# U3 h computed once in the reset gate's PSUM bank, copied into the update gate's bank, with both gates' message products added on top

## The chip, the cores and the metric

The kernel runs on one core of a Trainium2 chip. The metric is the device time of one execution in microseconds, as the median of several executions. Everything is in one launch; the inputs are `x` (16 x 1024 x 128), a symmetric 0/1 adjacency matrix `adj` (1024 x 1024) and the weights, all fp32.

## The reference, cut to what matters

Layer 0 is a graph attention layer with a residual and a layer normalization; the change doesn't touch it. Layer 1 is a gated graph network: five steps, each of which replaces the state `h` of every batch, and then a residual and a layer normalization.

```python
def step(h, _):
    m_in = jnp.einsum('nm,bmd->bnd', in_matrix, h)      # adj
    m_out = jnp.einsum('nm,bmd->bnd', out_matrix, h)    # adj too: m_in == m_out
    av = jnp.concatenate([m_in, m_out], axis=-1)
    u3 = h @ u3_w.T + u3_b
    z = jax.nn.sigmoid(av @ w3_w.T + w3_b + u3)
    r = jax.nn.sigmoid(av @ w4_w.T + w4_b + u3)
    hv = jnp.tanh(av @ w5_w.T + w5_b + (r * h @ u5_w.T + u5_b))
    h = (1.0 - z) * h + z * hv
```

The term `u3` is the same in both gates.

## The kernel before

**Tiling.** The state of a batch is held transposed, as `hT`: 128 features on the partitions, 1024 nodes along the free axis, worked on in two halves of 512 (`e` = 0, 1). A half is one PSUM bank of 128 x 512 fp32. Since both adjacency matrices are `adj`, the kernel makes `m = adj h` once and adds the two halves of each gate's weight into `wm` (three 128 x 128 blocks: z, r, candidate) at the start. The sigmoids are made as tanh of half the argument, so the tanh takes `scale=0.5` and half the bias (`bh`), and the kernel works with r' = tanh and (r' + 1) h; the missing factor is in `u5h`, half of U5.

**One step of one batch** (`step(b, s)`), for each half, with the lines of the profile:

- L878: 16 products with `adj` add up the message into the bank `ps_acc` (the state, in node order, is split into two parts of a shorter format, `hN`, so that there are 2 x 8 of them); L896: ScalarE copies the bank to SBUF, as `m`.
- L908: the U3 product, from `hT`, into a bank of its own (`ps_g_u`); L911: ScalarE moves it to SBUF as `u`, with the bias of U3 added.
- L918: the message products of r and z from `m`, each into a bank (`ps_g_r`, `ps_g_z`); L921: VectorE adds `u` to each and writes the sum to SBUF; L924: ScalarE takes the tanh, in place.
- L932: VectorE makes (r + 1) h. L938 and L939: TensorE makes the candidate, the message part first and then the part of r h, in one bank (`ps_g_v`); L942: ScalarE takes its tanh, `hv`.
- L949, L956, L963: VectorE makes the new half of `hT` from `hv`, `z` and the old one.
- The new state has to be turned back to node order for the next step. L478: VectorE transposes blocks of 32 x 32; L483: SP's queue issues four DMAs that write it to a buffer D in DRAM, L487: one that reads it back as F; L497 (ScalarE, a cast) and L501 (VectorE, a subtraction) split F into the two parts of `hN` for the next adj products. For the last step of the last three batches, and some tiles of the first two, TensorE transposes instead (L468).

An fp32 product of this size takes two passes on TensorE, an adj product one.

Layer 0 of a batch: products of `x` with the weights (L524), one attention column (`pb`), 8 chunks of weighted sums on VectorE (L678), adj products of their own (L749, L805), a layer normalization (L441 to L455: VectorE, GpSimd, ScalarE), and the same turns through DRAM.

**The order of work** is not written out by hand. Each operation is given to a planner (`Plan.add`) with its engine, a length in nanoseconds, a rank, and what it reads and writes. Ranks come from batch and step (`rank_of(b, s)`: 5b + 3s, with other values for the last two batches, so that about two batches are in their steps at a time and another's layer 0 lies between) plus an offset from the table `D` (for the gates 0.2, for their sums 0.3 and 0.5, for the candidate 0.4, for a split 0.8). `Plan.order()` then plays the engines through, once, when the kernel is built: an engine that is free takes the ready operation of lowest rank for whose tiles there is still a buffer. Buffers are counted by kind in `kinds`; "ps" stands for the eight PSUM banks, shared by all products. The result is one fixed order for each engine, which is emitted as it is. On the chip an engine works through its list strictly in that order, and waits where an input isn't there yet. A change of the planner's operations or buffer counts can therefore move any instruction.

Planned lengths and allowances (`R` an adj product, `F` an fp32 product of 512 columns, `V` a VectorE and `A` a ScalarE operation, in ns):

```python
R, F, TR, V, A = 233, 858, 109, 605, 640
LAG = {"PE": 250, "DVE": 150, "ACT": 170, "POOL": 200, "SP": 2500, "DMA": 2400}
```

At the start TensorE has nothing to do for a few microseconds, and runs `IDLE` = 24 groups of four transposes of the identity (`idle_`, L396), of lowest rank.

Of the kernel before, what the change touches and what calls it, by code (L numbers as in the profile page):

```python
# [9 lines left out]
F32 = mybir.dt.float32  # L10
F32R = mybir.dt.float32r
I32 = mybir.dt.int32
AF = mybir.ActivationFunctionType
ALU = mybir.AluOpType
AX = mybir.AxisListType

P = 128
N = 1024
HALF = 512
# [106 lines left out]
def kernel(  # L126
# [52 lines left out]
    nc = tc.nc  # L179
    B = x_t.shape[0]  # L180

    const = ctx.enter_context(tc.tile_pool(name="const", bufs=1))
    PS = bass.MemoryType.PSUM
# [4 lines left out]
    wm = const.tile([P, 3, P], F32, tag="wm", name="wm")  # L188
    u3 = const.tile([P, P], F32, tag="u3", name="u3")
    u5 = const.tile([P, P], F32, tag="u5", name="u5")  # L190
    u5h = const.tile([P, P], F32, tag="u5h", name="u5h")
    bias = const.tile([P, 5], F32, tag="bias", name="bias")
    bh = const.tile([P, 2], F32, tag="bh", name="bh")
    b5 = const.tile([P, 1], F32, tag="b5", name="b5")
    ident = const.tile([P, P], F32, tag="ident", name="ident")
    shift = const.tile([P, 1], F32, tag="shift", name="shift")
    ones = const.tile([P, 2], F32, tag="ones", name="ones")
    mhalf = const.tile([P, NC], F32, tag="mhalf", name="mhalf")
    att2 = const.tile([P, 2], F32, tag="att2", name="att2")

    seen = const.tile([P, B, NC + 4], F32, tag="seen", name="seen")
# [4 lines left out]
    def exact(pools):  # L206

        def pool(name, bufs, space=None):
# [7 lines left out]
        kinds = {  # L216
            "xt": (2, [P, N], F32, None),
            "hx": (2, [P, NC, P + 3], F32, None),
            "pb": (1, [P, N], F32, None),
            "hl": (2, [P, 2, NC, P], F32R, None),  # L220
            "yT": (1, [P, N], F32, None),
            "part": (1, [P, HALF], F32, None),
            "junk": (1, [P, HALF], F32, None),
            "y0": (4, [P, NC, P], F32, None),
# [2 lines left out]
            "T": (3, [P, HALF], F32, None),  # L227
            "F": (3, [P, HALF], F32, None),
            "m": (4, [P, HALF], F32, None),
            "u": (3, [P, HALF], F32, None),  # L230
            "r": (3, [P, HALF], F32, None),
            "z": (3, [P, HALF], F32, None),
            "hv": (2, [P, HALF], F32, None),
# [10 lines left out]
            "rstd": (3, [P, 2, 4], F32, None),  # L244
            "D": (6, [P, HALF], F32, bass.MemoryType.DRAM),
            "ud": (2, [3, N], F32, bass.MemoryType.DRAM),
            "ps": (8, [P, HALF], F32, PS),
        }
        places = {tag: pool(f"{tag}_p", k[0], k[3]) for tag, k in kinds.items()}
        tiles = {}  # L250
# [1 line left out]
        def T(t, dtype=None, shape=None):  # L252
            if t not in tiles:
                _, sh, dt, _ = kinds[t[0]]
                tiles[t] = places[t[0]].tile(
                    shape or sh, dtype or dt, tag=t[0], name="_".join(map(str, t)).replace("-", "n")
                )
            return tiles[t]
# [14 lines left out]
        R, F, TR, V, A = 233, 858, 109, 605, 640  # L273

        def pe(*a, **k):
            plan.add("PE", *a, **k)

        def dve(*a, **k):
            plan.add("DVE", *a, **k)

        def act(*a, **k):
            plan.add("ACT", *a, **k)
# [5 lines left out]
        D = dict(m=0, pu=0, u=0, pr=0.2, pz=0.2, sr=0.3, r=0.3, pv=0.4, sz=0.5, z=0.5, hv=0.6, h=0.6, tr=0.6, split=0.8)  # L288
# [13 lines left out]
        boot = ("hl", "boot")  # L302
# [5 lines left out]
        ws = ("T", "ws")  # L308
# [40 lines left out]
        def lands(pieces, what):  # L349
            plan.add("DMA", 190 * pieces, -103, lambda: None, writes=what)  # L350
# [7 lines left out]
        for k in range(NC // 2):  # L358
            lands(8, [(staged[k], 1)])
        lands(9, [(boot, "ws"), (("xt", 1), 0), (("xt", 1), 1)])  # L360
        lands(10, [(boot, "late"), (("u",), 0), (ws, "b")])

        def constants():
            make_identity(nc, ident)
            nc.gpsimd.memset(shift, -SHIFT)
            nc.gpsimd.memset(ones, 1.0)
            nc.gpsimd.memset(mhalf, -0.5)

        plan.add("POOL", 2000, -100, constants, writes=[(("ident",), 0), (("ones",), 0)])

# [23 lines left out]
        def idle_():  # L394
            for j in range(4):
                nc.tensor.transpose(T(("ps", "idle"))[:, j * P : (j + 1) * P], ident, ident)  # L396

        for i in range(IDLE):
            pe(4 * TR, 9000, idle_, reads=[(("ident",), 0)], writes=[(("ps", "idle"), 0)])

# [3 lines left out]
        def sums():  # L404
            w = W("w345").rearrange("p (j t e) -> p j t e", j=3, t=2)
            nc.vector.tensor_tensor(wm, w[:, :, 0, :], w[:, :, 1, :], ALU.add)
            nc.vector.tensor_tensor(b5, bias[:, 2:3], bias[:, 4:5], ALU.add)
            nc.vector.tensor_scalar(u5h, u5, 0.5, None, ALU.mult)
            nc.vector.tensor_scalar(bh, bias[:, 0:2], 0.5, None, ALU.mult)

        def own_weights():
            pb_ = ("ps", "g", "b")
            pe(150, -4.6, lambda: column_(pb_, slice(2 * P, 3 * P), 5), reads=[(ws, "b"), (("rz", 0), 1)], writes=[(pb_, 0)])
            dve(160, -4.3, lambda: nc.vector.tensor_copy(bias, T(pb_)[:, 0:5]), reads=[(pb_, 0)], writes=[(("bias",), 0)])
            dve(270, -4.5, self_, reads=[(boot, "ws"), (("ident",), 0), (("zs", 0), NC - 1)], writes=[(("wsi",), 0)])
            dve(1000, -4.2, sums, reads=[(boot, "late"), (("bias",), 0), (("u",), 0), (("rz", 0), 1)], writes=[(("wm",), 0)])

        def adj_tables(c):
            st = staged[c // 2]
# [448 lines left out]
        def step(b, s):  # L868
            rank = rank_of(b, s)
            hT, hN, y0 = ("hT", b), ("hN", b, s), ("y0", b)  # L870
            hs = [slice(0, HALF), slice(HALF, N)]
            for e in range(2):
                pm, m = ("ps", "acc", b, s, e), ("m", b, s, e)

                def pm_(e=e, pm=pm):
# [18 lines left out]
                    writes=[(pm, 0)],  # L894
# [2 lines left out]


            for e in range(2):
                m, u, r, z, hv = (k + (b, s, e) for k in (("m",), ("u",), ("r",), ("z",), ("hv",)))  # L900
                pu, pr, pz, pv = (("ps", "g", b, s, e, k) for k in ("u", "r", "z", "v"))
                mark = (("after",), b, s, e)

                def h(e=e):
                    return T(hT)[:, hs[e]]

                def pu_(pu=pu, h=h):
                    nc.tensor.matmul(T(pu), u3, h(), start=True, stop=True)  # L908

                def u_(pu=pu, u=u):  # L910
                    nc.scalar.activation(T(u), T(pu), AF.Identity, bias=bias[:, 3:4], scale=1.0)  # L911

                pe(F, rank + D["pu"], pu_, reads=[(hT, e), (("u",), 0)], writes=[(pu, 0), mark])
                act(A, rank + D["u"], u_, reads=[(pu, 0), (("bias",), 0)], writes=[(u, 0)])
                for p_, t, j, due in ((pr, r, 1, 'r'), (pz, z, 0, 'z')):

                    def gate_(p_=p_, j=j, m=m):
                        nc.tensor.matmul(T(p_), wm[:, j, :], T(m), start=True, stop=True)  # L918

                    def sum_(p_=p_, t=t, u=u):  # L920
                        nc.vector.tensor_tensor(T(t), T(p_), T(u), ALU.add)  # L921

                    def sig_(t=t, j=j):
                        nc.scalar.activation(T(t), T(t), AF.Tanh, bias=bh[:, j : j + 1], scale=0.5)  # L924

                    pe(F, rank + D["p" + due], gate_, reads=[(m, 0), mark, (("wm",), 0)], writes=[(p_, 0)])
                    dve(V, rank + D["s" + due], sum_, reads=[(p_, 0), (u, 0)], writes=[(t, 0)])
                    act(A, rank + D[due], sig_, reads=[(t, 0)], writes=[(t, 1)])
                dve(
                    V,  # L930
                    rank + D["r"],
                    lambda r=r, h=h: nc.vector.scalar_tensor_tensor(T(r), T(r), 1.0, h(), ALU.add, ALU.mult),  # L932
                    reads=[(r, 1), (hT, e)],
                    writes=[(r, 2)],
                )

                def pv_(pv=pv, m=m, r=r):
                    nc.tensor.matmul(T(pv), wm[:, 2, :], T(m), start=True, stop=False)  # L938
                    nc.tensor.matmul(T(pv), u5h, T(r), start=False, stop=True)  # L939

                def hv_(pv=pv, hv=hv):
                    nc.scalar.activation(T(hv), T(pv), AF.Tanh, bias=b5, scale=1.0)  # L942

                pe(2 * F, rank + D["pv"], pv_, reads=[(m, 0), (r, 2), (("wm",), 0), (("u",), 0)], writes=[(pv, 0)])
                act(A, rank + D["hv"], hv_, reads=[(pv, 0), (("wm",), 0)], writes=[(hv, 0)])
                dve(
                    V,
                    rank + D["h"],
                    lambda hv=hv, h=h: nc.vector.tensor_tensor(T(hv), T(hv), h(), ALU.subtract),  # L949
                    reads=[(hv, 0), (hT, e)],  # L950
                    writes=[(hv, 1)],
                )
                dve(
                    V,
                    rank + D["h"],
                    lambda hv=hv, z=z: nc.vector.scalar_tensor_tensor(T(hv), T(z), 1.0, T(hv), ALU.add, ALU.mult),  # L956
                    reads=[(hv, 1), (z, 1)],
                    writes=[(hv, 2)],
                )
                dve(  # L960
                    V,
                    rank + D["h"],
                    lambda hv=hv, h=h: nc.vector.scalar_tensor_tensor(h(), T(hv), 0.5, h(), ALU.mult, ALU.add),  # L963
                    reads=[(hv, 2)],
                    writes=[(hT, e)],
                )
# [376 lines left out]
```

## Time and profile before

| | before |
|---|---|
| median of 3 executions | 1528.85 us (1527.25 to 1529.43) |
| profiled execution, its own time | 1530.39 us |
| its span in the trace | 1528.6 us |
| granted TensorE clock, mean | 0.993 |
| TensorE (PE) busy | 1497.9 us, 98%, 5200 instructions |
| VectorE (DVE) busy | 1171.3 us, 77%, 2757 |
| ScalarE (ACT) busy | 841.6 us, 55%, 1656 |
| GpSimd (POOL) busy | 141.0 us, 9%, 265 |
| share of the chain that ended last | PE 87%, DMA 4%, DVE 3%, POOL 2%, ACT 2% |

How to read it: the busy time of an engine is the time in which it worked on an instruction, waits not counted. PE is the products and PEld the loading of their weights, which goes on beside them. The span goes from the first to the last recorded event; the execution's own time is 1.79 us longer than the span. The chain is followed backwards from the last instruction, at each step to whatever let it start. In a row of groups, "out<-in" are the tile names without their numbers, then sizes and types, then how many; after the bar stand the group's busy time in us and the mean of one in ns; then the engine's idle time just ahead of it and what ended most of that. In a timeline row stand the start in us, the length in us, engine, line, operation and tiles; SPq is SP's DMA queue.

### The profile page before, as it was taken

To read this page: it belongs to the slowest core of one execution; us is meant where nothing else is said; L and a number is where in the kernel's file an instruction comes from. 1 tells how busy PE (TensorE), PEld (TensorE's weight loads), DVE (VectorE), ACT (ScalarE), POOL (GpSimd) and SP (SyncE) were. 2 spreads that over 40 slices of the span, in tenths; PEclk is the share of its full clock that TensorE was granted. 3 is DMA by queue.
4 is the path that set the end of the run, shared out by engine and by line. 5 is a ranking of instruction groups with operands and counts; after the bars stand their busy time and mean duration, and the time that the engine had idled before them with its cause. 6 is when DMAs were issued, how large, how long until landed. Compare 5 with 4: busy or idle time off the path is not lost.

```text
span 1528.6 us, 17756 instructions
## 1 busy us (share of the span) xinstructions
PE 1497.9 (98%) x5200; PEld 944.5 (62%) x5200; DVE 1171.3 (77%) x2757; ACT 841.6 (55%) x1656; POOL 141.0 (9%) x265
## 2 busy tenths in 40 slices
PE   8999999999999999999999999999999999999996
PEld 7656566666666666666666566666666666666663
DVE  5778787878787777877878778777877888776665
ACT  4564645566465655555566455655555565555544
POOL 0101001011110201111011110101111011000001
PEclk9999999999999999999999999999999999999998
DMA  4124344242433324334242433324334233322121
GB/s 171 30 81 124 89 124 122 87 119 84 117 90 97 104 63 130 85 96 129 67 124 74 118 91 97 104 62 127 88 98 124 64 88 111 104 75 78 42 74 38
DMA packets 193982, 144.83 MB, mean 95 GB/s; under 512 B 33279, under 2 KB 158934, under 8 KB 193878
## 3 DMA queue, kind: packets, MB, share of 16 engines
q1 hardware_dynamic: 193314, 142.78, 32.8%
q8 instruction: 42, 0.69, 0.2%
q10 hardware_dynamic: 564, 0.85, 0.2%
q14 instruction: 62, 0.51, 0.1%
HBM read 79.95 MB, written 63.61 MB: 94 GB/s over the span
## 4 chain that ended last, share of the span: by engine, by line
PE 87%; DMA 4%; DVE 3%; POOL 2%; ACT 2%; SPq 1%; issue 1%; POOLq 0%; DVEq 0%; ACTq 0%
PE ps_acc L878 36%; PE ps_g_r L918 8%; PE ps_g_u L908 8%; PE ps_g_v L938 8%; PE ps_g_v L939 8%; PE ps_g_z L918 8%; PE ps_acc_po L749 7%; PE ps_g_ph L524 1%; DMA F<-D 1%; DMA D<-T 1%; SPq L483 1%; DMA F_y<-D_y 1%; POOL rstd_y L448 1%; PE ps_acc_po L805 1%; ACT y L455 1%
## 5 line engine op out<-in xcount | busy, mean ns | idle before, releaser
L878 PE MATMUL ps_acc<-adj,hN 128*128 128x512 f32 x2560 | 668.9, 415 | 0.7 <-DVE hN L501 0.7
L878 PEld LDWEIGHTS ps_acc<-adj,hN 128*128 128x128 f32 x2560 | 479.9, 188 | 166.9 <-issue 55.2
L896 ACT COPY m<-ps_acc 128x512 f32<-128x512 f32 x160 | 92.9, 580 | 156.7 <-PE ps_acc L878 156.4
L501 DVE TENSOR_TENSOR hN<-F,hN 128x512 fp32r<-128x512 f32 x128 | 88.1, 689 | 116.3 <-ACT hN L497 115.9
L942 ACT ACTIVATE hv<-ps_g_v,b 128x512 f32<-128x512 f32 x160 | 109.8, 687 | 105.5 <-PE ps_g_v L939 105.4
L918 PE MATMUL ps_g_r<-m,wm 128*128 128x512 f32 x320 | 164.4, 595 | 3.6 <-ACT m L896 3.6
L938 PE MATMUL ps_g_v<-m,wm 128*128 128x512 f32 x320 | 164.3, 595 | 3.4 <-ACT u L911 3.4
L939 PE MATMUL ps_g_v<-r,u5h 128*128 128x512 f32 x320 | 164.4, 595 | 0.3 <-DVE r L932 0.3
L918 PE MATMUL ps_g_z<-m,wm 128*128 128x512 f32 x320 | 163.4, 592 | 0.0
L497 ACT CAST hN<-F 128x512 fp32r<-128x512 f32 x128 | 79.1, 619 | 135.5 <-DMA F<-D 135.2
L921 DVE TENSOR_TENSOR r<-ps_g_r,u 128x512 f32<-128x512 f32 x160 | 109.0, 683 | 58.3 <-PE ps_g_r L918 55.0
L908 PE MATMUL ps_g_u<-hT,u 128*128 128x512 f32 x320 | 152.7, 598 | 0.7 <-ACT hT L861 0.7
L924 ACT ACTIVATE r<-r,bh 128x512 f32<-128x512 f32 x160 | 114.8, 721 | 67.5 <-DVE r L921 66.3
L949 DVE TENSOR_TENSOR hv<-hv,hT 128x512 f32<-128x512 f32 x160 | 109.5, 685 | 55.1 <-ACT hv L942 54.3
L749 PE MATMUL ps_acc_po<-adj,hl 128*128 128x512 f32 x512 | 145.5, 432 | 1.8 <-ACT hl L726 1.0
L749 PEld LDWEIGHTS ps_acc_po<-adj,hl 128*128 128x128 f32 x512 | 97.3, 190 | 42.1 <-issue 19.1
L924 ACT ACTIVATE z<-z,bh 128x512 f32<-128x512 f32 x160 | 113.0, 716 | 12.4 <-DVE z L921 11.6
L932 DVE SCALAR_TENSOR_TENSOR r<-r,hT 128x512 f32<-128x512 f32 x160 | 108.5, 681 | 12.7 <-ACT r L924 12.5
L911 ACT ACTIVATE u<-ps_g_u,bias 128x512 f32<-128x512 f32 x160 | 106.1, 682 | 17.5 <-PE ps_g_u L908 17.2
L956 DVE SCALAR_TENSOR_TENSOR hv<-z,hv 128x512 f32<-128x512 f32 x160 | 108.6, 680 | 3.4 <-ACT z L924 0.9
L921 DVE TENSOR_TENSOR z<-ps_g_z,u 128x512 f32<-128x512 f32 x160 | 108.5, 682 | 2.9 <-PE ps_g_z L918 2.0
L939 PEld LDWEIGHTS ps_g_v<-r,u5h 128*128 128x128 f32 x320 | 61.0, 191 | 77.7 <-issue 61.5
(132 smaller groups left out, 1482.5 us busy)
## 6 DMA issues: line engine op xcount, KB each, us to landing
D<-T SPq DMA_DIRECT2D x616, 64.0 KB
F<-D SPq DMA_DIRECT2D x154, 256.0 KB
out_dram<-o SPq DMA_DIRECT2D x32, 256.0 KB
xt<-in_x_dram SPq DMA_DIRECT2D x15, 512.0 KB
pb<-ud SPq DMA_DIRECT2D x14, 512.0 KB
D_y<-T_y SPq DMA_DIRECT2D x112, 64.0 KB
F_y<-D_y SPq DMA_DIRECT2D x28, 256.0 KB
D_b<-T_b SPq DMA_DIRECT2D x112, 64.0 KB
```

The lines of the kernel that those rows point to most:

```text
L749: nc.tensor.matmul(T(po), hl[:, k, c, :], adj[:, c, hs], start=(first and i == 0), stop=(last and i == len(terms) - 1),)
L878: nc.tensor.matmul(T(pm), T(hN)[:, k, c, :], adj[:, c, hs[e]], start=(c == 0 and k == 0), stop=(c == NC - 1 and k == 1),)
L908: nc.tensor.matmul(T(pu), u3, h(), start=True, stop=True)
L918: nc.tensor.matmul(T(p_), wm[:, j, :], T(m), start=True, stop=True)
L921: nc.vector.tensor_tensor(T(t), T(p_), T(u), ALU.add)
L924: nc.scalar.activation(T(t), T(t), AF.Tanh, bias=bh[:, j : j + 1], scale=0.5)
L932: lambda r=r, h=h: nc.vector.scalar_tensor_tensor(T(r), T(r), 1.0, h(), ALU.add, ALU.mult),
L938: nc.tensor.matmul(T(pv), wm[:, 2, :], T(m), start=True, stop=False)
L939: nc.tensor.matmul(T(pv), u5h, T(r), start=False, stop=True)
L942: nc.scalar.activation(T(hv), T(pv), AF.Tanh, bias=b5, scale=1.0)
L949: lambda hv=hv, h=h: nc.vector.tensor_tensor(T(hv), T(hv), h(), ALU.subtract),
L956: lambda hv=hv, z=z: nc.vector.scalar_tensor_tensor(T(hv), T(z), 1.0, T(hv), ALU.add, ALU.mult),
```

## The change

The U3 product of a half goes straight into the bank of the r gate. ScalarE copies it from there into the bank of the z gate; with that the copy to SBUF as `u` and its pool are gone. The message products of r and z no longer start a new sum in their banks (`start=False`), but add to what is there. The two additions on VectorE are removed, and the two tanhs read PSUM. The bias of U3, which the move to SBUF added, is now added to `bh` once at the start.

The z gates get two banks of their own ("gz"), and the common pool "ps" has six in place of eight. [...]two products of the identity with a tile of zeros (`fill_`) are run into the two "gz" banks once at the start, with `start=True`. GpSimd sets that tile of zeros. The r bank is started by the U3 product itself. The message products now also depend on the copy, r's as well as z's.

The table `D`, the planned lengths and everything of layer 0 are as before; only the key of the weights' landing is called "uw" instead of "u".

```diff
             "T": (3, [P, HALF], F32, None),
             "F": (3, [P, HALF], F32, None),
             "m": (4, [P, HALF], F32, None),
-            "u": (3, [P, HALF], F32, None),
...
-            "ps": (8, [P, HALF], F32, PS),
+            "ps": (6, [P, HALF], F32, PS),
+            "gz": (2, [P, HALF], F32, PS),
...
             nc.gpsimd.memset(mhalf, -0.5)
+            nc.gpsimd.memset(zeros, 0.0)
...
+        def fill_(k):
+            nc.tensor.matmul(T(("gz", "fill", k)), ident, zeros, start=True, stop=True)
+
+        for k in range(kinds["gz"][0]):
+            pe(F, -99, lambda k=k: fill_(k), reads=[(("ident",), 0)], writes=[(("gz", "fill", k), 0)])
...
-            nc.vector.tensor_scalar(bh, bias[:, 0:2], 0.5, None, ALU.mult)
+            nc.vector.tensor_tensor(bh, bias[:, 0:2], bias[:, 3:4].to_broadcast([P, 2]), ALU.add)
+            nc.vector.tensor_scalar(bh, bh, 0.5, None, ALU.mult)
...
-                m, u, r, z, hv = (k + (b, s, e) for k in (("m",), ("u",), ("r",), ("z",), ("hv",)))
-                pu, pr, pz, pv = (("ps", "g", b, s, e, k) for k in ("u", "r", "z", "v"))
+                m, r, z, hv = (k + (b, s, e) for k in (("m",), ("r",), ("z",), ("hv",)))
+                pr, pz, pv = ("ps", "g", b, s, e, "r"), ("gz", b, s, e), ("ps", "g", b, s, e, "v")
...
-                def pu_(pu=pu, h=h):
-                    nc.tensor.matmul(T(pu), u3, h(), start=True, stop=True)
-
-                def u_(pu=pu, u=u):
-                    nc.scalar.activation(T(u), T(pu), AF.Identity, bias=bias[:, 3:4], scale=1.0)
-
-                pe(F, rank + D["pu"], pu_, reads=[(hT, e), (("u",), 0)], writes=[(pu, 0), mark])
-                act(A, rank + D["u"], u_, reads=[(pu, 0), (("bias",), 0)], writes=[(u, 0)])
-                for p_, t, j, due in ((pr, r, 1, 'r'), (pz, z, 0, 'z')):
+
+                def pu_(pr=pr, h=h):
+                    nc.tensor.matmul(T(pr), u3, h(), start=True, stop=True)
+
+                def u_(pr=pr, pz=pz):
+                    nc.scalar.copy(T(pz), T(pr))
+
+                pe(F, rank + D["pu"], pu_, reads=[(hT, e), (("uw",), 0)], writes=[(pr, 0), mark])
+                act(A, rank + D["u"], u_, reads=[(pr, 0)], writes=[(pz, 0)])
+                for p_, t, j, due in ((pr, r, 1, "r"), (pz, z, 0, "z")):
 
                     def gate_(p_=p_, j=j, m=m):
-                        nc.tensor.matmul(T(p_), wm[:, j, :], T(m), start=True, stop=True)
-
-                    def sum_(p_=p_, t=t, u=u):
-                        nc.vector.tensor_tensor(T(t), T(p_), T(u), ALU.add)
-
-                    def sig_(t=t, j=j):
-                        nc.scalar.activation(T(t), T(t), AF.Tanh, bias=bh[:, j : j + 1], scale=0.5)
-
-                    pe(F, rank + D["p" + due], gate_, reads=[(m, 0), mark, (("wm",), 0)], writes=[(p_, 0)])
-                    dve(V, rank + D["s" + due], sum_, reads=[(p_, 0), (u, 0)], writes=[(t, 0)])
-                    act(A, rank + D[due], sig_, reads=[(t, 0)], writes=[(t, 1)])
+                        nc.tensor.matmul(T(p_), wm[:, j, :], T(m), start=False, stop=True, skip_group_check=True)
+
+                    def sig_(p_=p_, t=t, j=j):
+                        nc.scalar.activation(T(t), T(p_), AF.Tanh, bias=bh[:, j : j + 1], scale=0.5)
+
+                    pe(F, rank + D["p" + due], gate_, reads=[(m, 0), mark, (pz, 0), (("wm",), 0)], writes=[(p_, 1)])
+                    act(A, rank + D[due], sig_, reads=[(p_, 1)], writes=[(t, 1)])
```

In the changed kernel the same operations have these lines: adj products L888, copy of m L906, U3 product L919, the copy between the banks L922, gates L929, tanhs of r and z L932, (r + 1) h L939, candidate L945 and L946, its tanh L949, then L956, L963, L970; the turn L478, L493, L497; the split L507.

## The prediction

> **What bounds the kernel now.** I read the page's busy line first, then its slices, then the table by stage, then TensorE's waits.
>
> ```profile
> PE 1497.9 (98%) x5200; PEld 944.5 (62%) x5200; DVE 1171.3 (77%) x2757; ACT 841.6 (55%) x1656; POOL 141.0 (9%) x265
> PE   8999999999999999999999999999999999999996
> ```
>
> TensorE works through the whole span except the first and last slices. VectorE, from which the change takes work, has 23% to spare. The table by stage (length, PE busy, then the other engines) puts a number on it:
>
> ```profile
> 100.00:1400.00 1300.00, 1293.02 (x4400) 811.26 (x4399) 1021.74 (x2367) 727.22 (x1419) 120.41 (x216) 1.00 0.35 99
> 1510.00:1520.00 10.00, 3.77 (x14) 1.59 (x12) 8.09 (x26) 3.21 (x7) 1.17 (x2) 0.88 0.10 29
> ```
>
> In 1300 us TensorE is idle for 7.0 us; only the last 18 us belong to VectorE, ScalarE, GpSimd and the output DMA. The list of TensorE's waits (total, times, longest) tells what those 7 us are:
>
> ```profile
> PE ps_g_r L918 <- ACT m L896: 3.6, 5, 1.2
> PE ps_g_v L938 <- ACT u L911: 3.4, 1, 3.4
> ```
>
> 3.6 + 3.4 = 7.0: late copies of m, and one wait at 112.2 us for a PSUM bank still held by a U3 product. That is all that a faster gate can win in the body.
>
> The groups, by line (busy, mean ns, idle before):
>
> ```profile
> L921 DVE TENSOR_TENSOR r<-ps_g_r,u 128x512 f32<-128x512 f32 x160 | 109.0, 683 | 58.3 <-PE ps_g_r L918 55.0 <-ACT u L911 2.6 <-ACT r L924 0.2
> L921 DVE TENSOR_TENSOR z<-ps_g_z,u 128x512 f32<-128x512 f32 x160 | 108.5, 682 | 2.9 <-PE ps_g_z L918 2.0
> L924 ACT ACTIVATE r<-r,bh 128x512 f32<-128x512 f32 x160 | 114.8, 721 | 67.5 <-DVE r L921 66.3
> L911 ACT ACTIVATE u<-ps_g_u,bias 128x512 f32<-128x512 f32 x160 | 106.1, 682 | 17.5 <-PE ps_g_u L908 17.2
> L896 ACT COPY m<-ps_acc 128x512 f32<-128x512 f32 x160 | 92.9, 580 | 156.7 <-PE ps_acc L878 156.4
> L939 PE MATMUL ps_g_v<-r,u5h 128*128 128x512 f32 x320 | 164.4, 595 | 0.3 <-DVE r L932 0.3
> ```
>
> **What the Trainium skill says.** "PSUM — Partial Sum Buffer" (The four PSUM rules): ScalarE's writes do not touch a bank's written bits, and a product without the first-flag adds to what ScalarE wrote only where a product set the bit before. So the two fills are needed, once, and the additions in the banks can work; no row of this trace shows it. "Perfetto Trace Analysis" (Optimizing Scalar/DVE Operations): ScalarE's access costs about 93 ns on SBUF and 51 ns on PSUM. The trace agrees in sign: tanh from SBUF takes 721 ns, tanh from PSUM (L942) 687. "TensorE: Matmul & The Clock Gate" (Architectural detail): ScalarE and VectorE are strict first-in-first-out. The trace shows it at 725.45 us below: a tanh with its input ready stands behind a cast that waits for a DMA. My slow case rests on that.
>
> **The change, part by part.**
>
> *Removed from VectorE:* 320 additions x 0.682 us = 218 us of busy time. *Removed from ScalarE:* 320 tanhs now read PSUM, 320 x 0.03 = 10 us; 160 biased copies (682 ns) become plain copies from PSUM to PSUM. No row has that form. Nearest are the copy of m (580 ns, to SBUF) and L911 (682 ns); by the second page it may be 40 ns below 580. I take 0.58, keep 0.53 to 0.72: between 0 and 24 us less busy. In the body these gains lie beside a TensorE that doesn't stop, so they count nothing there.
>
> *TensorE:* 160 U3 products and 320 gate products as before. Adding instead of overwriting costs nothing: L939 adds (595 ns a pass), L938 starts a group (595 ns too). The fills are two fp32 products, four passes, 0.86 us each at full clock (four passes of L908 fill 105.01 to 106.73 us, 1.72), at most 3.5 us at half clock. In the new order they take the place of 16 of the 20 idle transposes before the attention column (20 in 4.43 us), the rest of the idle transposes move to about 18 us. They must wait for GpSimd's new 128x512 memset: the 128x128 one takes 0.20 us, so 0.2 to 0.8 (four times the elements). Cover: the column's result, ready at 7.07 us, is read at 8.89, behind a cast that waits for adj. Slack 1.8 us; without it, up to 0.8 us.
>
> *One more small VectorE operation* on the biases (0.15 us near 28 us) lies under the 4.84 us of L749: nothing.
>
> *Moved:* a U3 product now owns its r bank until tanh, and 6 + 2 banks replace 8, so the planner reorders TensorE. I laid the two emitted orders beside each other with 0.86 us for an fp32 product and 0.233 us for an adj product. Median TensorE work between a U3 product and its r gate: 1.72 us before, 5.45 after; the least is 1.30, against 0.1 + 0.58 + 0.1 us for the copy, so the new wait of the gates is covered. Between the product for m and the r gate: 8.9 before, 12.3 after, and the usual 3.43 us of the second half mostly becomes 5 or more; four of the five m waits go (2.4 us; the one near 147 us keeps 1.72). At 112 us the eight products with adj no longer stand ahead of the waiting one: 3.4 us go. Body: **-5.8 us**, bounds -7 and -2.
>
> *Start, 60 to 90 us:* the longer-held banks push two of the four h products and one wsi product (0.9 + 0.86 us) of batch 3 out of a stretch where TensorE waits anyway (1.67 and 0.65 us), into the full part. Against that, the second candidate product of batch 0 comes 1.8 us earlier, and so the DMA round trip behind the 0.65 us wait. I take **+1**, bounds -1.5 and +2.5.
>
> *Added wait.* The gates now wait for the copy. Behind a waiting gate stands all of TensorE, so the 5.45 and 1.30 us above are its only cover; a copy that takes 1.1 us would show at the 1.30 us sites alone. On ScalarE the copy stands where L911 stood, so the copies of m and the tanhs behind it wait no longer than before.
>
> *Tail.* Before, VectorE was late with the additions, and TensorE, then ScalarE, with them:
>
> ```profile
> 1509.65 1.13 PE L939 MATMUL ps_g_v<-r,u5h 128*128 128x512 f32 x2 [0.26 <-DVE r L932]
> ...
> 1510.12 0.68 DVE L921 TENSOR_TENSOR z<-ps_g_z,u 128x512 f32<-128x512 f32 x1
> ...
> 1511.26 0.70 ACT L924 ACTIVATE z<-z,bh 128x512 f32<-128x512 f32 x1
> ...
> 1511.87 1.34 ACT L942 ACTIVATE hv<-ps_g_v,b 128x512 f32<-128x512 f32 x2
> ```
>
> The candidate's product ends near 1510.8, but its tanh (L942) starts at 1511.87, behind that z tanh (0.61 us), and the product itself was 0.26 late: 0.26 + 0.61 = **-0.9** without the additions. What stays ahead is the layernorm's scaling on ScalarE (1.63 us from 1509.72), so it may be only -0.3. After 1512.57 VectorE works without a gap, so what is won there reaches the end.
>
> *The site that may lose.* Once per batch (ten periods, in step 3 of a batch) TensorE's cover shrinks. This is the timeline of one period before:
>
> ```profile
> 718.90 3.77 SPq L483 DMA_DIRECT2D D<-T  x8
> ...
> 722.15 8.02 PE L878 MATMUL ps_acc<-adj,hN 128*128 128x512 f32 x32
> ...
> 722.83 1.57 SPq L487 DMA_DIRECT2D F<-D  x2
> ...
> 725.45 0.62 ACT L497 CAST hN<-F 128x512 fp32r<-128x512 f32 x1 [2.83 <-DMA F<-D]
> 725.98 0.72 ACT L924 ACTIVATE r<-r,bh 128x512 f32<-128x512 f32 x1
> ```
>
> The gates end at 722.15, and 32 adj products keep TensorE busy until 730.0, when the candidate's product needs r times h. The second r tanh waits behind a cast, the cast for the DMA round trip of another batch's state; r times h is late by nothing because of the 32. In the new order one group of 16 stands ahead of the gates, and the candidate's product follows 3.44 us after the r gate. Count from the end of the other batch's candidate product, 712.1 here. That product now falls due at +15.2 us (TensorE work in the new order). Before, the cast came 13.0 to 13.4 us after the tanh that follows that end in six of eight periods that I looked at, 14.5 in two. In ScalarE's new order the cast, the copy of m, the tanh and, on VectorE, r times h follow each other: 0.62 + 0.57 + 0.72 + 0.69 + 0.15 for a wake-up = 2.75. On SP's queue four issues of D, not eight, now stand ahead of the first F, which takes 0 to 0.8 us off the cast (half of 3.77 is 1.9, but F also waits for D to land). With 13.1 - 0.8 = 12.3 r times h is ready at 15.05: no stall in eight periods, 1.25 in two, 2.5 us in all. With nothing off: 8 x 0.65 + 2 x 2.05 = 9.3. I take the middle, **+5**, bounds 0 and 15.
>
> *Batches 14 and 15* (1249 to 1478 us), where two batches overlap less: several sites there keep 3.43 us as cover, and one asks for the adj product 12.3 us after its source, where the round trip took 11.5 before (1483.9 to 1495.4). **+1**, bounds 0 and 4.
>
> **Sum.** -5.8 + 1 - 0.9 + 5 + 1 = +0.3. The profiled execution took 1530.39 us (span 1528.6 and 1.79 around it), 1.54 above the median of three, so 1530.7 for such an execution, and **1529.2** for the median.
>
> **The rivals.**
> - *Faster, nothing lost:* body and tail give -6.7, that is 1522.2. For it: VectorE loses 19% of its work, and each shown wait of m shrinks. Against: it needs the start and all ten periods to cost nothing, with 0.15 us of slack in the usual one.
> - *Slower, the cast decides:* if the cast comes at +13.9 (0.8 us later than usual before, as with a busier SP queue), each period stalls 1.5 us: 15 in place of 5, so +10.3, 1539.2. It decides from a mean stall of 0.8 us, a cast at +13.2. For it: before shows 13.1 as the usual value. Against: the shorter run of issues ahead of F.
> - *The copy from bank to bank is dear:* at 0.72 us it is covered everywhere (1.30); only beyond 1.1 us does it cost, some tenths. Time as forecast.
> - *It doesn't do what it says:* were the written bits not set, the gates would overwrite U3's part: same instructions, same time. The time can't tell.
>
> **How the numbers follow.** A difference within 0.2% (3.1 us) is about what a measurement of this kernel can tell from none. No change has 0.41, and holds the forecast with its own range 1525.8 to 1531.9. Slower has 0.37: the site's bounds reach much farther up than the gains reach down, since only 7 us can be won at all. Faster has 0.22. The range 1521.8 to 1540 takes in the faster case, and the slower one to a stall of 1.6 us a period.
>
> **What would show it.** In the profile after: VectorE near 953 us busy (1171 - 218); the copy between 0.53 and 0.72 us; TensorE's waits for m gone but for one, and the 3.4 us at the bank gone; instead a wait of L946 for r (L939), ten times, 0.25 us in most: below 0.1 makes the faster case, above 0.8 the slower. It is wrong in kind if the gates wait for the copy, if TensorE's busy time changes by over 3 us, or if the end moves apart from the body.

## The result: 14 us slower, and the profile after

The changed kernel takes 1542.88 us (median of 4, 1539.03 to 1543.98) against 1528.71 us before: ratio 1.0089, 95% interval 1.007 to 1.0109. The forecast was 1529.2 with a range up to 1540, so it was wrong; the rival in which the cast decides said 1539.2 and came nearest. The profiled execution took 1543.68 us, span 1541.8, 13.2 more than the span before.

The busy line of the changed kernel's page:

```profile
PE 1501.8 (97%) x5204; PEld 947.1 (61%) x5204; DVE 991.0 (64%) x2438; ACT 813.3 (53%) x1656; POOL 150.3 (10%) x266
```

VectorE lost 180 us of work (1171.3 to 991.0; the removed additions were 217.5 by their own lengths, but instructions on an engine overlap at their ends, and busy time counts the overlap once). The time did not follow. TensorE's waits (total, times, longest) say where it went:

```profile
PE ps_g_v L946 <- DVE r L939: 12.9, 11, 2.4
PE ps_g_ph L534 <- ACT y L465: 4.6, 1, 4.6
PE ps_acc_px L801 <- ACT y L465: 2.1, 1, 2.1
PE gz_fill L402 <- POOL zeros L369: 1.9, 1, 1.9
PE ps_g_r L929 <- ACT gz L922: 0.7, 2, 0.3
```

The 3.6 us for m and the 3.4 us for a bank that the kernel before had between 100 and 1400 us are gone, as forecast. In their place the candidate product waits for r 12.9 us, eleven times. Ten of these waits are alike, once in a batch from 365 to 1201 us, 10.5 us in all; this is the site of the prediction. The eleventh is another:

```profile
242.79 1.17 PE L946 MATMUL ps_g_v<-r,u5h 128*128 128x512 f32 x2 [2.35 <-DVE r L939]
```

There the tanh of r is done at 239.84, but (r + 1) h starts at 242.06, because of what VectorE has in front of it: an operation that waits until 240.37 for a DMA of a piece of `adj` (`look`), another on that piece, and the subtraction of a split. At the start, h products (L534) and one wsi product (L801) wait for a bank: what releases them is ScalarE's layernorm scaling (L465), which reads the transposed y out of PSUM. The table by stage (length, PE busy, then the other engines; the clock is the third number from the end):

```profile
40.00:60.00 20.00, 17.21 (x53) 11.32 (x54) 9.77 (x34) 11.10 (x32) 1.36 (x3) 0.74 0.00 0
80.00:90.00 10.00, 7.91 (x24) 6.44 (x25) 4.62 (x14) 5.95 (x16) 1.63 (x4) 0.50 0.32 79
100.00:1400.00 1300.00, 1286.32 (x4385) 807.33 (x4384) 858.33 (x2083) 696.69 (x1413) 129.36 (x216) 1.00 0.36 99
```

TensorE is idle for 13.7 us between 100 and 1400 us, where it was 7.0. In each of the two stretches with a wait for a bank the granted clock falls to half for a while: 0.74 in the mean from 40 to 60 us (0.91 before), 0.50 from 80 to 90 (1.00 before).

The span's 13.2 us divide so: +6.6 us of idle TensorE in the body (12.9 + 0.7 - 7.0); -0.8 in the tail (idle after the last candidate product: 2.11 + 0.74 + the last 11.4 us, where it was 2.75 + 0.77 + 11.3, and a wait of 0.26 ahead of it that is gone); the rest, **+7.4**, is put down to the start. The profile agrees with that size: before 100 us TensorE is idle for 3.4 us more than in the kernel before (12.1 and 8.7), and the clock stands at half for 20.5 us in place of 6.8.

One of the ten periods in the timeline of the changed kernel:

```profile
724.47 2.85 SPq L1013 DMA_DIRECT2D out_dram<-o  x2
...
725.27 1.65 ACT L465 ACTIVATE o<-o,rstd_o 128x128 f32<-128x128 f32 x4 [0.24 <-POOL rstd_o L460]
...
725.70 0.70 DVE L488 STREAM_TRANSPOSE T<-hT 128x512 f32<-128x512 f32 x1
...
727.43 1.93 SPq L493 DMA_DIRECT2D D<-T  x4
...
733.58 0.62 ACT L507 CAST hN<-F 128x512 fp32r<-128x512 f32 x1 [4.82 <-DMA F<-D]
...
734.59 0.69 ACT L932 ACTIVATE r<-ps_g_r,bh 128x512 f32<-128x512 f32 x1
...
736.19 1.12 PE L946 MATMUL ps_g_v<-r,u5h 128*128 128x512 f32 x2 [1.53 <-DVE r L939]
```

Read it upwards. L946 is 1.53 us late: it waits for (r + 1) h, which VectorE makes from 735.45 to 736.14. The r gate's product (L929) was in the bank by about 731.2, but its tanh starts at 734.59, because ScalarE has a cast in front of it that waits for F. F was read late (issued at 730.74) because D was written late. The block to write, T, is there at 726.40, but D is issued at 727.43: on SP's queue two output DMAs of an old batch stand before it, the second of which waits until ScalarE ends that batch's scaling at 726.92. So the last layernorm of an old batch holds up the r gate of another.

The same two output DMAs stood ahead of D in the kernel before, too. In the period that the prediction shows they did no harm, because the scaling ended at 718.18, before T was there (718.86), and D went out at 718.90:

```profile
716.11 2.47 SPq L1006 DMA_DIRECT2D out_dram<-o  x2
...
716.53 1.65 ACT L455 ACTIVATE o<-o,rstd_o 128x128 f32<-128x128 f32 x4
...
718.16 0.70 DVE L478 STREAM_TRANSPOSE T<-hT 128x512 f32<-128x512 f32 x1
```

In most periods D waited behind them already there, for 0.4 to 1.6 us after T; in the changed kernel it waits in all ten, for 1.0 to 2.0 us.

The changed operations themselves were as cheap as forecast (busy, mean ns):

```profile
L922 ACT COPY gz<-ps_g_r 128x512 f32<-128x512 f32 x160 | 89.9, 570 | 25.1 <-PE ps_g_r L919 24.8
L932 ACT ACTIVATE r<-ps_g_r,bh 128x512 f32<-128x512 f32 x160 | 109.9, 689 | 29.0 <-PE ps_g_r L929 28.6 <-DVE T L488 0.2 <-DVE hT L970 0.2
```

The copy from bank to bank takes 570 ns, the tanh from PSUM 689, where it was 721 from SBUF. The gates waited for the copy 0.7 us in all.

### The profile page after: what moved, and what is told of

It reads as the page before. It is cut to its first block, busy times and chain, and to the rows that moved or that the text cites. A ratio compares the mean times of both kernels' runs of the same rounds, so it can differ in the third digit from the quotient of the medians.

```text
span 1541.8 us, 17536 instructions
## 1 busy us (share of the span) xinstructions
PE 1501.8 (97%) x5204; PEld 947.1 (61%) x5204; DVE 991.0 (64%) x2438; ACT 813.3 (53%) x1656; POOL 150.3 (10%) x266
## 4 chain that ended last, share of the span: by engine, by line
PE 60%; DMA 15%; DVE 10%; SPq 5%; ACT 4%; issue 3%; POOL 2%; ACTq 0%; DVEq 0%; POOLq 0%
PE ps_acc L888 24%; PE ps_acc_po L759 6%; PE ps_g_v L946 6%; PE ps_g_r L919 6%; PE ps_g_r L929 6%; PE gz L929 5%; PE ps_g_v L945 5%; DMA F<-D 5%; SPq L493 4%; DMA D<-T 3%; DMA uu<-ud 2%; DMA F_y<-D_y 1%; DVE hv L956 1%; DVE T L488 1%; DVE hv L963 1%
## 5 line engine op out<-in xcount | busy, mean ns | idle before, releaser
L888 PE MATMUL ps_acc<-adj,hN 128*128 128x512 f32 x2560 | 686.4, 420 | 0.7 <-ACT y L465 0.7
L888 PEld LDWEIGHTS ps_acc<-adj,hN 128*128 128x128 f32 x2560 | 483.7, 189 | 176.4 <-issue 65.1
L507 ACT CAST hN<-F 128x512 fp32r<-128x512 f32 x128 | 79.1, 618 | 221.7 <-DMA F<-D 221.5
L906 ACT COPY m<-ps_acc 128x512 f32<-128x512 f32 x160 | 93.1, 583 | 177.8 <-PE ps_acc L888 177.8
L946 PE MATMUL ps_g_v<-r,u5h 128*128 128x512 f32 x320 | 164.6, 596 | 12.9 <-DVE r L939 12.9
L956 DVE TENSOR_TENSOR hv<-hv,hT 128x512 f32<-128x512 f32 x160 | 109.3, 683 | 104.8 <-ACT hv L949 104.6
L929 PE MATMUL ps_g_r<-m,wm 128*128 128x512 f32 x320 | 163.8, 593 | 0.8 <-ACT gz L922 0.7
L945 PE MATMUL ps_g_v<-m,wm 128*128 128x512 f32 x320 | 163.4, 592 | 0.0
L929 PE MATMUL gz<-m,wm 128*128 128x512 f32 x320 | 163.4, 592 | 0.0
L949 ACT ACTIVATE hv<-ps_g_v,b 128x512 f32<-128x512 f32 x160 | 109.0, 685 | 86.7 <-PE ps_g_v L946 86.1
L919 PE MATMUL ps_g_r<-hT,u 128*128 128x512 f32 x320 | 153.9, 601 | 0.7 <-ACT hT L871 0.7
L939 DVE SCALAR_TENSOR_TENSOR r<-r,hT 128x512 f32<-128x512 f32 x160 | 109.6, 687 | 58.1 <-ACT r L932 57.6
L759 PE MATMUL ps_acc_po<-adj,hl 128*128 128x512 f32 x512 | 138.5, 421 | 0.3 <-DVE hl L742 0.3
L932 ACT ACTIVATE r<-ps_g_r,bh 128x512 f32<-128x512 f32 x160 | 109.9, 689 | 29.0 <-PE ps_g_r L929 28.6
L759 PEld LDWEIGHTS ps_acc_po<-adj,hl 128*128 128x128 f32 x512 | 96.1, 188 | 36.3 <-issue 14.4
L946 PEld LDWEIGHTS ps_g_v<-r,u5h 128*128 128x128 f32 x320 | 59.9, 190 | 93.3 <-issue 58.1
L932 ACT ACTIVATE z<-gz,bh 128x512 f32<-128x512 f32 x160 | 108.8, 686 | 6.8 <-PE gz L929 6.8
L970 DVE SCALAR_TENSOR_TENSOR hT<-hv,hT 128x512 f32<-128x512 f32 x160 | 108.4, 678 | 5.3
L963 DVE SCALAR_TENSOR_TENSOR hv<-z,hv 128x512 f32<-128x512 f32 x160 | 107.9, 675 | 2.1
L488 DVE STREAM_TRANSPOSE T<-hT 128x512 f32<-128x512 f32 x154 | 108.4, 705 | 1.2
L929 PEld LDWEIGHTS gz<-m,wm 128*128 128x128 f32 x320 | 60.8, 190 | 76.5 <-issue 76.5
```

Of the source, the lines that this page charges most:

```text
L488: nc.vector.transpose(T(t).rearrange("p (b c i) -> p b c i", b=4, c=4), turned(src()))
L759: nc.tensor.matmul(T(po), hl[:, k, c, :], adj[:, c, hs], start=(first and i == 0), stop=(last and i == len(terms) - 1),)
L888: nc.tensor.matmul(T(pm), T(hN)[:, k, c, :], adj[:, c, hs[e]], start=(c == 0 and k == 0), stop=(c == NC - 1 and k == 1),)
L919: nc.tensor.matmul(T(pr), u3, h(), start=True, stop=True)
L929: nc.tensor.matmul(T(p_), wm[:, j, :], T(m), start=False, stop=True, skip_group_check=True)
L932: nc.scalar.activation(T(t), T(p_), AF.Tanh, bias=bh[:, j : j + 1], scale=0.5)
```

## The experiments

Two theories stood against each other. **Order:** the time is lost by where the planner put instructions (the cast before the tanh, D behind an output DMA) and by the six banks at the start. **Operations:** gates that add up in PSUM and wait for a copy are late in themselves. Each run was timed beside the kernel before on its own chip (medians there 1525.75 to 1526.96), so ratios are compared.

**Six banks alone, in the kernel before.**

```diff
-            "ps": (8, [P, HALF], F32, PS),
+            "ps": (6, [P, HALF], F32, PS),
```

> The kernel before, with six banks for "ps" in place of eight and nothing else (the two other banks lie idle). Theory A, the loss at the start is the bank count: TensorE's waits for a bank held by a transposed y (ScalarE's layernorm scaling) appear before 100 us, some 4 to 7 us in all with the lower clock after them, and none of the once-per-batch stalls of the candidate product: about 1533 to 1536. Theory B, the loss at the start comes from the fills and the gates' new dependencies: no such waits, within 2 us of before.

Measured: 1533.62 us against 1526.11, ratio 1.0046 (1.0033 to 1.006), some 7 us. Four of its waits of TensorE:

```profile
PE ps_g_v L938 <- ACT u L911: 3.8, 1, 3.8
PE ps_t_b L468 <- ACT hT L861: 2.2, 1, 2.2
PE ps_acc_px L791 <- ACT y L455: 2.1, 1, 2.1
PE ps_g_ph L524 <- ACT y L455: 1.4, 1, 1.4
```

The wait of 3.8 us lies at 164.5 us and has its like in the kernel before (3.4); the other three lie before 100 us. The wait of 2.1 us for px is the one of the changed kernel, and the h products wait again; the candidate product waits for r only 0.3 us in all. From 100 to 1400 us TensorE is idle for no longer than before (5.2 us, 7.0 before). So taking two banks away costs about as much at the start as the change does (+7.4), and does not make the stalls of the periods. The pinch is not quite the same: here the U3 product still has a bank of its own, and z takes its bank from the six.

**The cast behind the tanh,** in the changed kernel. `later` moves one operation in the finished order, with all that depends on it.

```diff
-            for i in plan.order():
+            order = plan.order()
+            for b in range(1, 12):
+                order = later(plan, order, seat["cast", b + 1, 2, 0], seat["r", b, 3, 1])
+            for i in order:
```

> The changed kernel; in ScalarE's order the cast of hN (first half) is moved behind the r tanhs of (b, step 3) in the eleven periods, nothing else. Theory A, the tanh is late only because it stands behind a cast that waits for a DMA: the waits of the candidate product for r (12.9 us in 11) fall below 1 us in all, the time falls by 10 to 13 to about 1531. Theory B, r is late because of the additions in PSUM themselves (copy, gate wait): the waits stay, less than 3 us changes.

Measured: 1527.49 us against 1526.11, ratio 1.0005 (0.9993 to 1.0016). Beside the 1.0091 of the changed kernel (repeated below) that is 13 us less, some 10 of which the waits in the body account for. TensorE's waits from 100 to 1400 us:

```profile
PE ps_g_v L964 <- DVE r L957: 2.2, 1, 2.2
PE ps_g_r L946 <- ACT gz L939: 1.4, 3, 0.6
```

All ten waits of the candidate product in the periods are gone; the one that is left, at 241.7 us, is the other site, which this edit doesn't touch. That is why more than the 1 us expected remains. Every gate and copy is as it was. ScalarE's order differs in the place of eleven casts, and with them ten of the subtractions that need a cast (the split's second part) stand later in VectorE's order, where they stood ahead of (r + 1) h. The run therefore frees both queues of the wait for F, and does not tell ScalarE's share from VectorE's.

**The output DMA behind D,** in the changed kernel: the cast stays in front of the tanh.

```diff
+            order = plan.order()
+            for b in range(0, 11):
+                order = later(plan, order, seat["out", b, 1], seat["D", b + 2, 1, 0])
```

> The changed kernel; on SP's queue the second output DMA of an old batch is moved behind the four D issues of (b+2, step 1, first half), nothing else; ScalarE's order stays, the cast ahead of the tanh. Theory A, D is issued late because it stands behind an output DMA that waits for ScalarE's scaling of a layernorm: D goes out some 0.8 us earlier, F and the cast with it, and most stalls (median 0.8 us) go: 7 to 12 us less, 1531 to 1536. Rival: the cast is late for another reason (the round trip itself, VectorE's transpose): the stalls stay within 3 us.

Measured: 1529.04 us against 1526.11, ratio 1.0023 (1.0014 to 1.0031), some 10 us less than the changed kernel. The same period in its timeline:

```profile
716.59 1.78 SPq L509 DMA_DIRECT2D D<-T  x4
...
718.48 0.40 SPq L1031 DMA_DIRECT2D out_dram<-o  x1
...
722.49 0.62 ACT L524 CAST hN<-F 128x512 fp32r<-128x512 f32 x1 [3.56 <-DMA F<-D]
...
725.10 1.13 PE L963 MATMUL ps_g_v<-r,u5h 128*128 128x512 f32 x2
```

D is issued 2.06 us after the start of the other batch's second candidate tanh (714.53); in the changed kernel it was 3.08 (724.35 to 727.43). The whole chain moves up by that 1.0 us, and L963 starts without a wait. Over the body it waits 2.2 us, three times, 1.8 of them at the other site (239.7 us). Only the place of ten output DMAs differs, on SP's queue alone. So there are two links, and taking out either one is enough.

**One number of the planner,** in the changed kernel.

```diff
-            plan.add("POOL", 2200, rank, power, reads=[(mv, 0)], writes=[(rstd, 0)])
+            plan.add("POOL", 3000, rank, power, reads=[(mv, 0)], writes=[(rstd, 0)])
```

> The changed kernel, with one number of the planner: GpSimd's part of a layernorm is planned with 3000 ns in place of 2200 (measured in this trace, from the first of its four operations to the end of the last: about 3.0 us). If the losses are matters of the planned order, not of the additions in PSUM, a plan that knows of the late layernorm places both the cast and the start otherwise: once-per-batch stalls gone, fewer waits before 100 us, 1522 to 1530. If the operations themselves cost the time, it stays above 1538.

Measured: 1519.32 us against 1526.11, ratio 0.9951 (0.9937 to 0.9965), better than I expected. TensorE's only wait from 100 to 1500 us:

```profile
PE ps_t_u L573 <- ACT u L558: 1.6, 1, 1.6
```

In the order that the planner finds with this number neither the ten stalls nor the two long waits at the start arise, with the same operations and the same banks; TensorE never waits for a gate, a copy or an r in the body. The number is not simply the real length: GpSimd's four operations took 3.02 us in the period above, but 2.6 us in the mean of the changed kernel. The run shows that another order is free of the losses, not that 3000 is the right length.

**The changed kernel again.**

> The changed kernel once more, unaltered, as the partner of the three others here on the same chip. From its first measurement: slower than before by 0.7 to 1.1%, some 11 to 17 us.

Measured: 1539.99 us against 1525.75, ratio 1.0091 (1.0074 to 1.0109). The candidate product waits 11.5 us, nine times: 2.0 us at the other site and 9.5 in eight of the ten periods. The order is the same, yet single periods differ between the two executions by up to 0.75 us. The largest such difference, at 633 us, comes from the issue of D: 7.03 us after the candidate's tanh in the first execution, 6.12 in this one.

**The same number in the kernel before.** The diff is that of the fourth run.

> The kernel before, with the same number of the planner as in the run with 3000 ns for GpSimd's part of a layernorm, nothing else. If that number only mends what the change disturbed, the kernel before gains little, at most 4 us (its waits before 100 us and the 3.4 us for a bank at 112 us may move); if it is worth as much to the kernel before, 5 us or more, and the changed kernel has no lead at equal planning.

Measured: 1521.41 us against 1525.75, ratio 0.9966 (0.9955 to 0.9978): 4.3 us by the medians, 5.2 by the ratio. That lies on the border of what I had set, and so it is undecided between the two readings. The interval also overlaps that of the changed kernel with the same number (0.9937 to 0.9965), so at this equal planning a lead of the changed kernel is not shown either. Its start gains (clock 1.00 from 40 to 100 us), and a wait of 3.5 us stays in the body.

**Two planner numbers in the kernel before.**

```diff
-    LAG = {"PE": 250, "DVE": 150, "ACT": 170, "POOL": 200, "SP": 2500, "DMA": 2400}
+    LAG = {"PE": 250, "DVE": 150, "ACT": 170, "POOL": 200, "SP": 2800, "DMA": 2400}
...
-            plan.add("POOL", 2200, rank, power, reads=[(mv, 0)], writes=[(rstd, 0)])
+            plan.add("POOL", 2600, rank, power, reads=[(mv, 0)], writes=[(rstd, 0)])
```

> The kernel before, with two planner allowances: 2600 ns in place of 2200 for GpSimd's part of a layernorm, and 2800 in place of 2500 for the lag after an SP issue. A question to the method: does planning alone give the kernel before what the changed kernel gains with its new number? If the additions on VectorE bound the body, TensorE stays idle for 5 us or more between 100 and 1400 us and the time stays above 1523; if the order alone does, the idle falls below 2 us and the time to 1514 to 1521.

Measured: 1519.28 us against 1525.75, ratio 0.9955 (0.9938 to 0.9973). TensorE's waits from 100 to 1500 us:

```profile
PE ps_g_r L918 <- ACT m L896: 1.9, 1, 1.9
PE ps_g_v L939 <- DVE r L932: 0.8, 2, 0.5
```

2.4 us of these lie before 1400 us, over the 2 that I had set, but the time is inside the range for the order. The kernel before, with its 320 additions on VectorE, gets all but 2.4 us of its body by planning alone.

**Both numbers in the changed kernel:** 3000 for the layernorm, 3200 for the lag after an SP issue.

> The changed kernel with 3000 ns for GpSimd's part of a layernorm and 3200 for the lag after an SP issue. No once-per-batch stalls either way; it is to show whether there is anything left in the order: 1515 to 1520. If it stays at the time with 3000 alone, the body is exhausted and only start and tail remain.

Measured: 1516.96 us against 1525.75, ratio 0.9943 (0.9928 to 0.9959): the fastest version here, ahead of both kernels. Its body in the table by stage:

```profile
100.00:1400.00 1300.00, 1299.49 (x4441) 818.07 (x4440) 873.98 (x2089) 717.54 (x1417) 129.39 (x216) 1.00 0.36 100
```

0.5 us idle in 1300: the body is exhausted. The two numbers are not those of the kernel before (2600 and 2800), and the two intervals overlap, so a gain of the change itself at good planning is not shown.

**TensorE kept busy in the long wait at the start,** in the changed kernel.

```diff
+                def put_():
+                    nc.tensor.transpose(T(put)[0 : 3 * NC, 0:P], T(u).rearrange("p t c -> p (t c)"), ident)
+                    for k in range(40 if b == 2 else 0):
+                        nc.tensor.transpose(T(put)[:, (1 + k % 3) * P : (2 + k % 3) * P], ident, ident)
```

> The changed kernel; behind the small transpose of batch 2's attention row (the last work of TensorE before its 4.6 us wait at 76.8 us) TensorE gets 40 transposes of the identity (about 4.4 us), into columns of that bank that nobody reads, and nothing else. The wait for the bank stays where it was, TensorE only isn't idle in it. Theory A, the lower granted clock between 80 and 90 us (mean 0.50) comes from that idle stretch: it is 1.0 there, the 32 adj products behind it take 8.0 us in place of 10.0, and the time falls by 2 to 3 us. Theory B, the clock falls for another reason: still about 0.5 and 10 us there, no change in time. The similar dip from 42 to 52 us stays in both cases.

Measured: 1534.97 us against 1526.96, ratio 1.0055 (1.0034 to 1.0076). Stage and timeline of that run:

```profile
80.00:90.00 10.00, 8.71 (x41) 6.96 (x42) 6.50 (x18) 4.93 (x13) 0.00 (x0) 1.00 0.23 54
```

```profile
74.02 4.53 PE L574 MATMUL ps_t_u<-ident 128*128 128x128 f32 x40
...
81.92 7.73 PE L894 MATMUL ps_acc<-adj,hN 128*128 128x512 f32 x32 [1.28 <-ACT y L465]
```

The clock stays at 1.00 there, and the 32 adj products take 7.7 us, not the 10.0 of the changed kernel (from 85.06 on). The drop at 80 us came from the idle stretch. The gain is larger than the 2 to 3 us expected; in the profiled execution the dip around 50 us was shorter as well (0.91 from 40 to 60 us, 0.74 in the changed kernel). This edit doesn't touch it, and the run with the output DMA behind D, whose start is that of the changed kernel, shows 0.91 too. That part is not separated.

Not tried: seven banks with one for z, and a start that keeps eight banks until the first gates.

## Why the prediction was wrong

- **Removed work, price of the copy, tanh from PSUM, fills:** as forecast. The copy's 570 ns lies in the stated 530 to 720, though only 10 ns below the copy of m, where the prediction thought 40 possible. The memset took 0.53 us (0.2 to 0.8 forecast); with it the fills start at 1.93 us, but the first adj products of a step start at 47.79 us, where it was 49.07. VectorE's 991 us in place of 953 is the overlap told above. TensorE's busy time rose by 3.9 us, over the 3 that were to be a sign of an error in kind; products at half clock take longer (32 adj products 10.0 us where a part of them ran at half clock, 8.0 at full clock), and the clock was not in the sum.
- **Body:** -5.8 forecast, bounds -7 and -2; measured -6.3 (all 7.0 us of the old waits gone, 0.7 for the copy). The number is right, in part by luck. In the trace the wait for a bank ends at 158.65 us, not at 112.2, and no adj products stand just ahead of it; the waits for m end at 353.6, 503.3, 686.7, 870.2 and 1145.4 us, none near 147. So the reason given for the 3.4 us, and the site named for the wait of m that was to stay, belong to other places.
- **Tail:** -0.9 forecast; -0.8 measured, by the same step.
- **The once-per-batch site:** the mechanism is the one named, the cast ahead of the tanh; the size was not. +5 forecast for ten periods, 10.5 measured in ten, 1.05 us each, so the mean stall is over the 0.8 us from which on the slower rival decides. The failed step is "With 13.1 - 0.8 = 12.3": the cast came 13.0 to 14.4 us after the candidate's tanh, 13.6 in the mean. The shorter run of issues did help as forecast: from D's first issue to the cast it is 6.15 us in the period above (727.43 to 733.58), where it was 6.55 (718.90 to 725.45). But the step took D's own issue to be as early as before. It counted D's issues and left out the two output DMAs ahead of them, the second of which waits for ScalarE's scaling and so for GpSimd. In the period above that scaling ends 7.39 us after the tanh (719.53 to 726.92), 6.03 in the one before (712.15 to 718.18), and D goes out after 7.90 us in place of 6.75. Moving that DMA alone gave back 10 us.
- **The other site,** at 242.8 us: 2.35 us, and nothing like it in the prediction.
- **The start:** +1 forecast, bounds -1.5 and +2.5; +7.4 measured, the largest error. The step that failed is the one that counted only the products pushed into the full part (1.76 us). It priced neither the wait of the next product for the bank itself (4.6 and 2.1 us) nor the half clock after it. With six banks the kernel before loses about the same.
- **Batches 14 and 15:** +1 forecast; no wait of TensorE there.
- **The sum:** the errors are 6.4 us at the start, 5.5 at the site, 2.4 at the other site, -0.5 in the body, -1 for the last batches and 0.1 in the tail: 12.9 together, the difference between the +0.3 of the sum and the 13.2 of the span. It closes because the start is what the other parts leave over. One slip in the working: the middle of 2.5 and 9.3 is 5.9, not 5.
- **The slower rival** came near in part by luck: it had 15 us at the site, more than the 10.5 measured, and the same +1 at the start.

## What to carry to other kernels

When a fixed order is replanned, follow the new order of every queue for one period back to a landing DMA, with everything that stands ahead of it, including what belongs to another batch; an instruction that waits passes its wait on to all behind it. Buffers that were taken away were paid for here where the pipeline fills, not where it is full, and only in some orders: price the wait for the buffer, and the clock after it. And before an engine that is off the path is relieved, see what the order alone is worth: here two planner numbers alone made the kernel before 0.45% faster, nearly as much as the 0.49% by which the changed kernel with one raised number is ahead of the kernel before as it stood.

## What the runs showed of the hardware

- TensorE's clock fell to half for 3.41, 6.83 or 10.24 us in every dip of these traces but that at the end of the program: one, two or three times 3.41. In the changed kernel it was low from 42.36 to 52.60 us, falling inside an idle stretch of 2.11 us with one of 1.25 shortly before, and from 79.91 to 90.14 us, in an idle stretch of 4.63 us. The three parts of 3.41 us had TensorE busy for 2.67, 2.75 and 3.41 us in the first, for 1.90, 2.74 and 3.40 in the second: the clock came back behind the first part without a pause. The Trainium skill, "TensorE: Matmul & The Clock Gate" (What's actually happening), gives about 3.4 us for either turn, of idleness for the fall and of sustained work for the rise. The rise agrees. The fall in the stretch of 4.63 us does too (3.1 us after its start), but the one in the stretch of 2.11 us came 1.4 us after its start, and in the kernel before the clock was low from 46.51 to 49.92 us though TensorE had been busy for 2.14 of the 3.41 us ahead of it, with no pause over 0.66 us. What sets off such a fall stays open. In other executions the first dip was shorter (0.83 from 40 to 60 us in the repeated run), which adds to their spread.
- GpSimd's four small operations of a layernorm, planned with 2.2 us, took 1.94 to 3.3 us in the body of the changed kernel (once 4.6, in the mean 2.6), and in the two periods shown 2.18 us (kernel before, from 711.76) and 3.02 us (changed, from 719.74). Raising the planned length changed which order the planner finds.
- A gate product that adds to what ScalarE copied into its bank takes 592 ns a pass (z, L929), as it did when it started a new sum (592, L918).
